# Cross-attention softmax on VectorE straight from PSUM: maximum and subtract without ScalarE's copy, and an earlier division

## The chip, the cores and the metric

The kernel runs on one core of a Trainium2 chip. Its time is the device time of one execution in microseconds (us). A core has TensorE (PE, matrix products into PSUM), VectorE (DVE), ScalarE (ACT), GpSimd (POOL, which works on SBUF only in this kernel) and SyncE (SP, which only issues DMAs). Each engine runs its own instructions in the order in which they stand, and engines wait for each other through semaphores.

## The reference

Four cross-attention models run one after the other on x (8 batches x 256 tokens x 128) and a context (8 x 64 x 64). The third, L2, holds most of the work and is where the change lies: six layers, each with a self-attention, a cross-attention and a feed-forward block, all with 16 heads of 64.

```python
def step(t, p):
    skv, sq, sow, sob, ckv, cq, cow, cob, w1, b1, w2, b2, pg, pb = p
    tn = _ln(t, norm_g, norm_b)
    t = _mha(tn, tn, skv, sq, sow, sob, tgt_mask) + t
    tn = _ln(t, norm_g, norm_b)
    t = _mha(src, tn, ckv, cq, cow, cob, src_mask) + t
    tn = _ln(t, pg, pb)
    t = t + (jax.nn.relu(tn @ w1 + b1) @ w2 + b2)
    return (t, None)
```

In the cross-attention each of the 256 queries of a batch looks at 64 keys per head: scores, mask, softmax over the 64 keys, weighted sum of values, output projection. The softmax subtracts each row's maximum, exponentiates, and divides by the row's sum.

## The kernel before

**Order of the work.** Nothing is scheduled by a tool. The kernel collects small functions with `at(tick, phase, fn)`; at the end it runs through the ticks in order, and in each tick by phase (lines 1312 to 1323), and ties every instruction of PE, DVE, ACT and POOL behind the one before it on the same engine. So a phase number fixes where an instruction stands in its engine's queue. DMAs on SP are outside this order.

**Layers.** A layer of L2 takes 48 ticks. The self-attention has 32, four per batch (`plan_sa`, line 891), and the cross-attention 16 from tick T_ca on, two per batch (`plan_ca`, line 1108), that is one tick per tile of 128 queries. The feed-forward block of batch b follows at T_ca + 2b + 7 (products L1161, activation L1166) and + 9 (products L1178, add L1182). The next layer's self-attention starts at T_ca + 16, and its normalisation and projections some ticks before, so the stages overlap.

**A tile of cross-attention** (`plan_weights_64`, lines 329 to 446, called with a mask) goes through these steps, for a tile that starts in tick k:

| step | place (tick, phase) | engine and line |
|---|---|---|
| scores | k, 1 | PE L356, L363 (mask): 128 x 1024 into PSUM (16 heads x 64 keys) |
| lower | k, 2 | ACT copies to SBUF, L372; DVE row maximum, L374; POOL subtracts, L375 |
| exps | k, 8 | ACT exponential in place, L381 |
| divide | k+1, 2.4 | DVE sum L385 and reciprocal L386; POOL multiplies, L387 |
| turn | k+2, 2.5 | DVE two 32 x 32 block transposes, L395 |
| sums | k+3, 3.0 | PE L429; then DVE adds bias and residual into t, L1145 |

The same function without a mask serves L0 (16 tiles), where exps comes at k+1 and there is no divide.

**Other work in these ticks.** `ahead` (line 843) prepares a normalised, transposed input for each block: moments of each row on DVE (L849 to L855), their scales on POOL (L859, L862), the normalised rows xn either on ACT (L868) or on DVE (L873), then the transposes on PE (L882) and their eviction on ACT (L884). Its argument `on_scalar` picks the engine of xn; with ACT two small instructions more are needed, `mneg` (L855, DVE) and `nm` (L862, POOL). Self-attention passes False (line 1029), cross-attention and feed-forward take True. For batch 0 of the next layer's self-attention xn is at T_ca + 11, phase 2.6, and its transposes in the same tick, phase 7.2; for batch 1 both are at T_ca + 15. Values (L318, evicted by ACT L324) come in even ticks at 3.2, keys of two batches (L1120, evicted by ACT L1126) at 3.7 in every fourth. The next layer's projections (L902, L921) start at T_ca + 12. Its first scores are L939 at T_ca + 16, phase 1, and VectorE's mask, add and row minimum of them L953, phase 2; ACT's exponential of them is L958.

**PSUM.** All PE results go into one pool of four buffers of two banks each (`two_banks`, tag `ps`). A result waits until the reader of the tile that held its buffer before is done: L372 frees the scores, L1145 the sums, L884 the transposes, L324 the values, L953 the self-attention's scores.

Of the kernel before, what the change touches and what calls it, by code (L numbers as in the profile page):

```python
# [12 lines left out]
ALU = mybir.AluOpType  # L13
AX = mybir.AxisListType
PSUM = bass.MemoryType.PSUM

P = 128
B, S, D = 8, 256, 128
M, DM = 64, 64
# [8 lines left out]
def tile_xattn_stack(ctx: ExitStack, tc: tile.TileContext, io, out: bass.AP):  # L28
    nc = tc.nc
# [21 lines left out]
    def tp_tile():  # L51
        return one_bank("tp")
# [4 lines left out]
    def big(tag, bufs=4, shape=(P, 1024), dtype=F32):  # L57

        return heap.tile(list(shape), dtype, tag=tag, name=uniq(tag), bufs=bufs)

    def sb(shape, tag, bufs=2, pool=None):
        return (pool or act).tile(shape, F32, tag=tag, name=uniq(tag), bufs=bufs)

    def sm(shape, tag):
        return small.tile(shape, F32, tag=tag, name=uniq(tag))
# [12 lines left out]
    def column(name):  # L78
        v = io[name]
        t_ = const.tile([v.shape[0], 1], F32, tag=name, name=name)  # L80
        nc.sync.dma_start(out=t_, in_=v.unsqueeze(1))
        return t_
# [71 lines left out]
    norm_g = column("L2_norm_g")  # L154
    norm_b = column("L2_norm_b")
# [129 lines left out]
    def tt(b):  # L285
        return t[:, QT * b : QT * (b + 1), :]
# [7 lines left out]
    def at(tick, phase, fn):  # L294
        plan.setdefault(tick, []).append((phase, fn))
# [33 lines left out]
    def plan_weights_64(tick, qt, qT, keys, values, mask, take):  # L329
# [39 lines left out]
        def lower():  # L369
            sc = tl.pop("sc")  # L370
            e = big("e", shape=(P, 16, M))
            nc.scalar.copy(e.rearrange("p h k -> p (h k)"), sc)  # L372
            m = sm([P, 16], "m16")
            nc.vector.tensor_reduce(m, e, AX.X, ALU.max)  # L374
            nc.gpsimd.tensor_tensor(  # L375
                e, e, m.unsqueeze(2).to_broadcast([P, 16, M]), ALU.subtract
            )
            tl["e"] = e

        def exps():  # L380
# [53 lines left out]

        at(tick, 1, scores)
        at(tick, 2, lower)
        if mask is None:
            at(tick + 1, 2.05, exps)
            at(tick + 1, 2.5, turn)
            at(tick + 2, 1.9, sums_by_head)  # L440
            at(tick + 2, 4.6, outputs)
        else:
            at(tick, 8, exps)
            at(tick + 1, 2.4, divide)
            at(tick + 2, 2.5, turn)
            at(tick + 3, 3.0, sums)

# [235 lines left out]
    def plan_l0(b, T):  # L683
# [88 lines left out]
        for qt in range(QT):  # L772
            plan_weights_64(
                T + qt, qt, lambda: st["q"], lambda: st["k"], lambda: st["VW"], None,
                lambda ps, qt=qt: add(qt, ps),
            )
# [66 lines left out]
    def ahead(b, stats_at, normal_at, tT_at, g, bias, st, on_scalar=True):  # L843

        def moments():
            st["mv"] = sm([P, QT, 2], "mv")
            for j in range(QT):
                six = sm([P, 6], "six")
                nc.vector.bn_stats(six, tt(b)[:, j, :])  # L849
                nc.vector.bn_aggr(st["mv"][:, j, :], six)  # L850
            st["ve"] = sm([P, QT], "ve")
            nc.vector.tensor_scalar(st["ve"], st["mv"][:, :, 1], 1e-5, None, ALU.add)
            if on_scalar:
                st["mneg"] = sm([P, QT], "mneg")
                nc.vector.tensor_scalar(st["mneg"], st["mv"][:, :, 0], -1.0, None, ALU.mult)  # L855

        def scales():
            st["rstd"] = sm([P, QT], "rstd")
            nc.gpsimd.tensor_tensor(st["rstd"], st["ve"], mhalf, ALU.pow)  # L859
            if on_scalar:  # L860
                st["nm"] = sm([P, QT], "nm2")
                nc.gpsimd.tensor_tensor(st["nm"], st["mneg"], st["rstd"], ALU.mult)  # L862

        def normal():
            st["xn"] = sb([P, QT, D], "xn", 3)
            for j in range(QT):
                if on_scalar:
                    nc.scalar.activation(  # L868
                        st["xn"][:, j, :], tt(b)[:, j, :], AF.Identity,
                        scale=st["rstd"][:, j : j + 1], bias=st["nm"][:, j : j + 1],  # L870
                    )
                else:
                    nc.vector.tensor_scalar(  # L873
                        st["xn"][:, j, :], tt(b)[:, j, :], st["mv"][:, j, 0:1],
                        st["rstd"][:, j : j + 1], ALU.subtract, ALU.mult,
                    )

        def trans():
            ps = tp_tile()
            xn = st.pop("xn")  # L880
            for j in range(QT):
                nc.tensor.transpose(ps[:, j * P : (j + 1) * P], xn[:, j, :], ident)  # L882
            st["tT"] = sb([D, S], "tT", 5)
            nc.scalar.activation(st["tT"], ps[:, :S], AF.Identity, scale=g, bias=bias)  # L884

        at(*stats_at, moments)
        at(stats_at[0], 8.4, scales)
        at(*normal_at, normal)
        at(*tT_at, trans)

    def plan_sa(l, b, T):


        st = {"q": [], "k": [], "v": [], "oT": [], "eT": []}
# [131 lines left out]
        def mask():  # L1026
            st["nm"] = load_mask(b)

        ahead(b, (T - 6, 8.3), (T - 5, 2.6), (T - 5, 7.2), norm_g, norm_b, st, False)
        at(T - 2, -1, mask)  # L1030
        at(T - 4, 3.6, lambda: project(W["sa", l][2], "q", HD ** -0.5, 0, False))
        at(T - 4, 3.7, lambda: project(W["sa", l][2], "q", HD ** -0.5, 1, False))
# [75 lines left out]
    def plan_ca(l, b, T):  # L1108
# [38 lines left out]
        for qt in range(QT):  # L1147
            plan_weights_64(
                T + qt, qt, lambda: st["tT"], lambda: keys_of[b], lambda: st["VW"],
                nm2[:, b].unsqueeze(1).to_broadcast([P, 4, M]), lambda ps, qt=qt: add(qt, ps),  # L1150
            )
# [119 lines left out]
    for l in range(NL):  # L1271
        T_ca = T0 + 4 * B
        T_next = T_ca + 2 * B
        for b in range(B):
            plan_sa(l, b, T0 + 4 * b)
        plan_ca_weights(l, T_ca - 6)
        for b in range(B):
            plan_ca(l, b, T_ca + 2 * b)
            T_ff = T_ca + 2 * b + 7
            if l + 1 < NL:  # L1280
                plan_ff(l, b, T_ff, T_ff + 2)
            elif b < B - 2:
                plan_ff(l, b, T_ff, T_ff + 1)
            else:

                T_ff -= b - B + 3
                done = T_ca + 2 * b + 4
                plan_ff(
                    l, b, T_ff, T_ff + 1,
                    (4.6, (done, 6), (done, 8.7), (T_ff, 2.9)),  # L1290
                )
            T_end[b] = T_ff + 1
        if l > 0:
            at(T0 + 8, -1, lambda l=l: load_ff(l))
        if l + 1 < NL:
            at(T_ca + 4, -1, lambda l=l: load_sa(l + 1))
            at(T_next + 1, -1, lambda l=l: load_ca(l + 1))
        T0 = T_next
# [82 lines left out]
```

## Time and profile before

| what | value |
|---|---|
| median of three runs | 2408.54 us (2406.35 to 2409.7) |
| profiled execution | 2410.29 us; its span, first to last instruction, 2408.5 us |
| mean granted TensorE clock in it | 0.987 |
| L372, ACT copy of the scores (128 x 1024) | 112 times, mean 1006 ns |
| L374, DVE maximum | 112 times, mean 1217 ns |
| L375, POOL subtract | 112 times, mean 1902 ns |
| L381, ACT exponential | 112 times, mean 1062 ns |
| L385, L386, DVE sum and reciprocal | 96 times each, mean 1208 and 253 ns |
| L387, POOL multiply | 96 times, mean 1902 ns |
| L873, DVE xn (128 x 128) | 96 times, mean 562 ns |
| L868, ACT xn (128 x 128) | 192 times, mean 492 ns |

Of the 112 tiles 96 belong to the masked cross-attention (6 layers x 8 batches x 2). Busy time counts an engine's instructions from start to end; neighbours overlap a little, so a mean can exceed the advance from one start to the next. The chain of waits follows the work that ended last backwards, at each step to what released it. The timeline lists instructions by start time, runs of equal ones merged, with the idle time before them and its releaser in brackets.

### The profile page before, as it was taken

The numbers are of one execution on the slowest core, as the hardware profiler recorded it, in microseconds if no ns is written. First come the engines' busy times: TensorE is split into PE (matmuls) and PEld (weight loads), VectorE is DVE, ScalarE is ACT, GpSimd is POOL, SyncE is SP. The second block draws the span as 40 slices with busy tenths as digits, with TensorE's granted clock in tenths as the row PEclk, the third lists the DMA queues.
The fourth block names the chain that finished last, engine by engine and source line by source line (L and its number), as shares of the span: only waits on it lengthen the run. The fifth ranks groups of instructions, "written<-read, shape, count | busy, mean of one in ns | idle before, by whom it ended". The sixth has DMA issues, their size and how long they took to land.

```text
span 2408.5 us, 100346 instructions
## 1 busy us (share of the span) xinstructions
PE 2325.2 (97%) x42564; PEld 1719.9 (71%) x42564; DVE 1872.3 (78%) x6237; ACT 1707.7 (71%) x4514; POOL 1359.1 (56%) x2231
## 2 busy tenths in 40 slices
PE   7889999999999999999999999999999999999997
PEld 4557777777777777777777777777777777777775
DVE  5677887777888767888767888767888767888775
ACT  4567777667777667778667778667778667777663
POOL 2444556754556754555764555755555765455665
PEclk9989999999999999999999999999999999999998
DMA  6000022001022001012000012000013000001000
GB/s 180 2 2 20 21 73 65 2 3 30 21 64 66 11 3 30 21 56 73 12 2 26 21 45 87 12 2 18 25 40 89 21 2 18 25 26 42 2 4 16
DMA packets 102834, 76.90 MB, mean 32 GB/s; under 512 B 8113, under 2 KB 96881, under 8 KB 102386
## 3 DMA queue, kind: packets, MB, share of 16 engines
q1 hardware_dynamic: 101794, 70.16, 10.1%
q8 instruction: 335, 5.49, 0.9%
q14 instruction: 113, 0.93, 0.1%
q10 hardware_dynamic: 592, 0.33, 0.1%
HBM read 62.07 MB, written 8.39 MB: 29 GB/s over the span
## 4 chain that ended last, share of the span: by engine, by line
PE 75%; DVE 13%; ACT 5%; POOL 4%; issue 2%; DMA 0%; SPq 0%; POOLq 0%; ACTq 0%; DVEq 0%
PE sc L939 12%; PE mm L902 12%; PE mm L994 12%; PE mm L1012 6%; PE mm L921 6%; PE mm L429 6%; PE sc L356 5%; DVE e L953 3%; PE mm L1178 3%; PE mm L1161 3%; DVE eTc L978 2%; DVE m L374 2%; POOL e L968 2%; PE mm L1120 2%; PE mm L318 2%
## 5 line engine op out<-in xcount | busy, mean ns | idle before, releaser
L968 POOL TENSOR_SCALAR e<-e,rs 128x256 f32<-128x256 f32 x1536 | 702.8, 478 | 706.3 <-DVE rs L966 696.5
L958 ACT ACTIVATE e<-e,mn 128x256 f32<-128x256 f32 x1536 | 758.6, 495 | 151.3 <-DVE mn L953 146.5
L953 DVE CUSTOM_DVE_ANT_0 e<-sc,nm 128x256 f32<-128x256 f32 x1536 | 543.1, 419 | 93.4 <-PE sc L939 92.3
L978 DVE STREAM_TRANSPOSE eTc<-e 128x512 f32<-128x512 f32 x768 | 516.2, 694 | 59.4 <-POOL e L968 58.2
L939 PE MATMUL sc<-k,q 64*32 64x256 f32 x12288 | 380.8, 383 | 2.3 <-DVE o L299 1.3
L994 PE MATMUL mm<-eTc,v 32*64 32x256 f32 x12288 | 363.4, 378 | 5.7 <-ACT AT L1095 3.3
L375 POOL TENSOR_TENSOR e<-e,m 128x1024 f32<-128x1024 f32 x112 | 213.0, 1902 | 262.1 <-DVE m L374 262.1
L994 PEld LDWEIGHTS mm<-eTc,v 32*64 32x64 f32 x12288 | 277.1, 131 | 88.5 <-issue 22.2
L939 PEld LDWEIGHTS sc<-k,q 64*32 64x32 f32 x12288 | 221.8, 107 | 125.3 <-issue 51.4
L374 DVE TENSOR_REDUCE m<-e 128x16 f32<-128x1024 f32 x112 | 136.3, 1217 | 197.0 <-ACT e L372 197.0
L958 ACT ACTIVATION_READ_ACCUMULATOR e<-e,mn 128x1 f32 x1536 | 287.9, 187 | 0.0
L356 PE MATMUL sc<-q,tT 128*32 128x256 f32 x3072 | 217.0, 382 | 3.8 <-DVE t L1019 3.2
L429 PE MATMUL mm<-v,o 128*128 128x128 f32 x1536 | 197.5, 283 | 1.9 <-DVE t L1145 1.7
L429 PEld LDWEIGHTS mm<-v,o 128*128 128x128 f32 x1536 | 183.1, 195 | 19.0 <-issue 9.1
L902 PE MATMUL mm<-tT,w_sk 128*128 128x256 f32 x768 | 189.2, 389 | 0.2 <-PE mm L994 0.2
L1012 PEld LDWEIGHTS mm<-w_sow,o 128*128 128x128 f32 x1536 | 175.1, 192 | 17.6 <-issue 12.3
L921 PE MATMUL mm<-w_sv,tT 128*32 128x256 f32 x3072 | 185.6, 382 | 0.0
L1012 PE MATMUL mm<-w_sow,o 128*128 128x128 f32 x1536 | 183.6, 278 | 1.3 <-ACT WVO L1093 1.3
L387 POOL TENSOR_TENSOR e<-e,r 128x1024 f32<-128x1024 f32 x96 | 182.6, 1902 | 0.5 <-DVE r L386 0.5
L301 ACT COPY v<-mm 128x1024 f32<-128x1024 f32 x96 | 97.1, 1012 | 115.4 <-PE mm L921 115.4
L902 PE MATMUL mm<-tT,w_sq 128*128 128x256 f32 x768 | 173.6, 379 | 0.0
L902 PEld LDWEIGHTS mm<-tT,w_sk 128*128 128x128 f32 x768 | 138.3, 190 | 44.2 <-issue 29.2
(222 smaller groups left out, 3489.4 us busy)
## 6 DMA issues: line engine op xcount, KB each, us to landing
nm<-mask_d SPq DMA_DIRECT2D x192, 128.0 KB
wd<-o SPq DMA_DIRECT2D x48, 128.0 KB
w_sk<-in_L_sa_kv_dram SPq DMA_DIRECT2D x6, 512.0 KB
w_sv<-in_L_sa_kv_dram SPq DMA_DIRECT2D x24, 128.0 KB
w_sq<-in_L_sa_q_dram SPq DMA_DIRECT2D x6, 512.0 KB
w_sow<-in_L_sa_ow_dram SPq DMA_DIRECT2D x6, 512.0 KB
w_ckv<-in_L_ca_kv_dram SPq DMA_DIRECT2D x12, 256.0 KB
w_cq<-in_L_ca_q_dram SPq DMA_DIRECT2D x6, 512.0 KB
```

Source lines behind the costliest of these rows:

```text
L356: nc.tensor.matmul(sc[32 * a : 32 * a + 32, q, :], lhsT=qT()[:, qb * 32 : (qb + 1) * 32], rhs=keys()[:, a].rearrange("p h k -> p (h k)"), ...
L375: nc.gpsimd.tensor_tensor(e, e, m.unsqueeze(2).to_broadcast([P, 16, M]), ALU.subtract)
L429: nc.tensor.matmul(ps[:, :D], lhsT=eT[:, s].rearrange("p q x -> p (q x)"), rhs=vw[:, r, k, g, :], start=(s == 0), stop=(s == 7),)
L902: nc.tensor.matmul(ps[:, i * S : (i + 1) * S], lhsT=w[:, c * P : (c + 1) * P], rhs=st["tT"], start=True, stop=True,)
L921: nc.tensor.matmul(ps[32 * a : 32 * a + 32, i, :], lhsT=st["tT"][:, kb * 32 : (kb + 1) * 32], rhs=sv[:, a].rearrange("p g x -> p (g x)"), ...
L939: nc.tensor.matmul(sc[32 * a : 32 * a + 32, r, j, :], lhsT=st["q"][g][rows, a, qb * 32 : (qb + 1) * 32], rhs=st["k"][g][rows, a, :], start ...
L953: nc.vector.tensor_tensor_reduce(e[:, i, :], sc4[:, i, :], st["nm"][:, 2 * jj + i % 2, :], -1.0, 3.0 * BIG, ALU.add, ALU.min, mn[:, i : i ...
L958: nc.scalar.activation(e[:, i, :], e[:, i, :], AF.Exp, scale=-1.0, bias=mn[:, i : i + 1], accum_out=rs[:, i : i + 1],)
L968: nc.gpsimd.tensor_scalar(e[:, i, :], e[:, i, :], rs[:, i : i + 1], 1.0, ALU.mult, ALU.mult)
L978: nc.vector.transpose(eT[:, r, :, 2 * jj : 2 * jj + 2, :], e[:, 2 * r : 2 * r + 2, :].rearrange("p j (k x) -> p k j x", x=32),)
L994: nc.tensor.matmul(ops[a // 2][r * HD : (r + 1) * HD, a % 2, :S], lhsT=st["v"][kb // 4][rows, kb % 4, (2 * g + r) * HD : (2 * g + r + 1) * ...
L1012: nc.tensor.matmul(st["ps"][:, j * D : (j + 1) * D], lhsT=st["oT"][c // 4][:, c % 4, j * P : (j + 1) * P], rhs=sow[:, c, :], start=(c == 0 ...
```

## The change

For masked tiles `lower` no longer copies the scores to SBUF: VectorE takes the maximum from PSUM and subtracts it from PSUM, writing the difference to SBUF. ScalarE's copy and GpSimd's subtract go. L0's tiles keep the old way. `divide` moves from phase 2.4 of tick k+1 to phase 0.9, ahead of that tick's scores and lower. Batches 0 and 1 of each self-attention get their xn from ScalarE (`b < 2` as `on_scalar`). In the changed program the maximum is L381, the subtract L382, and the lines behind them are 7 higher.

```diff
         def lower():
             sc = tl.pop("sc")
             e = big("e", shape=(P, 16, M))
-            nc.scalar.copy(e.rearrange("p h k -> p (h k)"), sc)
             m = sm([P, 16], "m16")
-            nc.vector.tensor_reduce(m, e, AX.X, ALU.max)
-            nc.gpsimd.tensor_tensor(
-                e, e, m.unsqueeze(2).to_broadcast([P, 16, M]), ALU.subtract
-            )
+            if mask is None:
+                nc.scalar.copy(e.rearrange("p h k -> p (h k)"), sc)
+                nc.vector.tensor_reduce(m, e, AX.X, ALU.max)
+                nc.gpsimd.tensor_tensor(
+                    e, e, m.unsqueeze(2).to_broadcast([P, 16, M]), ALU.subtract
+                )
+            else:
+                sc = sc.rearrange("p (h k) -> p h k", k=M)
+                nc.vector.tensor_reduce(m, sc, AX.X, ALU.max)
+                nc.vector.tensor_tensor(
+                    e, sc, m.unsqueeze(2).to_broadcast([P, 16, M]), ALU.subtract
+                )
             tl["e"] = e
...
         else:
             at(tick, 8, exps)
-            at(tick + 1, 2.4, divide)
+            at(tick + 1, 0.9, divide)
             at(tick + 2, 2.5, turn)
             at(tick + 3, 3.0, sums)
...
-        ahead(b, (T - 6, 8.3), (T - 5, 2.6), (T - 5, 7.2), norm_g, norm_b, st, False)
+        ahead(b, (T - 6, 8.3), (T - 5, 2.6), (T - 5, 7.2), norm_g, norm_b, st, b < 2)
```

## The prediction

> **What bounds the kernel now.** I read the page first, then groups by line, then the timeline of one layer's cross-attention. A tile is 128 queries of one batch; I write tile k and tick k for the k-th of a layer's cross-attention (tick T_ca + k, 16 tiles), and give the times of layer 0, whose tick 0 starts at 396.7 us.
>
> The page's busy shares and its chain that ended last:
>
> ```profile
> PE 2325.2 (97%) x42564; PEld 1719.9 (71%) x42564; DVE 1872.3 (78%) x6237; ACT 1707.7 (71%) x4514; POOL 1359.1 (56%) x2231
> ...
> PE 75%; DVE 13%; ACT 5%; POOL 4%; issue 2%; DMA 0%; SPq 0%; POOLq 0%; ACTq 0%; DVEq 0%
> ```
>
> TensorE carries the chain. Time taken off another engine is worth only the PE idle that goes with it; time put on VectorE costs where PE waits for it. The three groups that the change touches (last columns: busy us, mean ns, idle before and what ended it):
>
> ```profile
> L375 POOL TENSOR_TENSOR e<-e,m 128x1024 f32<-128x1024 f32 x112 | 213.0, 1902 | 262.1 <-DVE m L374 262.1
> ...
> L374 DVE TENSOR_REDUCE m<-e 128x16 f32<-128x1024 f32 x112 | 136.3, 1217 | 197.0 <-ACT e L372 197.0
> ...
> L372 ACT COPY e<-sc 128x1024 f32<-128x1024 f32 x112 | 112.7, 1006 | 50.2 <-PE sc L363 25.4 <-PE sc L343 24.8
> ```
>
> The idle of 262 and 197 us is off the path: the waits view names hardly any PE wait on these lines. PE idles in the cross-attention at two places per layer, shown by the timeline (start, duration, engine, line, idle before). The first is tick 6:
>
> ```profile
> 430.94 1.21 DVE L374 TENSOR_REDUCE m<-e 128x16 f32<-128x1024 f32 x1
> ...
> 433.74 0.93 PE L882 MATMUL tp<-ident,xn 128*128 128x128 f32 x4 [1.19 <-ACT xn L868]
> ...
> 434.64 0.25 DVE L1145 TENSOR_TENSOR t<-mm,tb 128x128 f32<-128x128 f32 x1
> ...
> 434.95 2.95 PE L429 MATMUL mm<-v,o 128*128 128x128 f32 x16 [0.28 <-DVE t L1145]
> ```
>
> VectorE is here some 4 us behind PE: the add L1145 of tile 2 frees the PSUM buffer that tile 3's sums need. The sums then take 2.95 us where others take 2.05, because the windows view has the granted clock (next to last but two) at 0.59 after this idle:
>
> ```profile
> 436.00:440.00 4.00, 4.00 (x49) 2.73 (x50) 3.70 (x6) 1.41 (x4) 2.54 (x3) 0.59 0.00 0
> ```
>
> The second is tick 11, where PE waits for the next layer's first normalisation on VectorE:
>
> ```profile
> 475.97 2.11 DVE L873 TENSOR_SCALAR xn<-t,mv,rstd 128x128 f32<-128x128 f32 x2
> ...
> 477.54 0.30 PE L882 MATMUL tp<-ident,xn 128*128 128x128 f32 x1 [0.88 <-DVE xn L873]
> 478.00 0.28 DVE L1145 TENSOR_TENSOR t<-mm,tb 128x128 f32<-128x128 f32 x1
> 478.13 0.33 PE L882 MATMUL tp<-ident,xn 128*128 128x128 f32 x1 [0.29 <-DVE xn L873]
> ```
>
> **Price of the new operations.** The subtract from PSUM with a broadcast has a near row: L631, 128x1024 from PSUM plus a broadcast, 1.207 us. The maximum from PSUM: L1221 reduces 256 elements from PSUM in 0.41 us, as L502 does from SBUF (0.41), so I take L374's 1.22. Back to back an instruction advances VectorE by 1.14 (424.79 to 425.93), and 1.24 if the next needs its result (425.93 to 427.17). So lower costs VectorE 1.24 + 1.14 = 2.38 us a tile, 1.24 more than before; over 96 tiles +119 us (78% to 83% of the span). ScalarE loses 96 x 1.006 = 97 us, GpSimd 96 x 1.902 = 183 us. Alone this is nothing: 33.9 us of VectorE idle per layer (before L374) could hold the 16 x 1.24 = 19.8 us, if it lay at the right ticks.
>
> The rows L631 and L374 show no surcharge for reading PSUM. [...]
>
> **The walk.** Order on VectorE in tick k becomes: divide(k-1) 1.41, max and subtract(k) 2.38, turn(k-2) 1.17, add(k-3) 0.20, and in even ticks from 4 two sets of moments, 2.26. A pair of ticks costs 12.6 us (before: 10.1). PE needs 9.8 for ticks 4 and 5 (420.38 to 430.17), but about 15.5 once the feed-forward joins (453.3 to 468.8). So VectorE is the slower up to about tick 8 and PE after it. Against that, the loop copy-max-subtract-exp-copy over three engines (1.0 + 1.2 + 1.9 + 1.0) disappears, and subtract ends earlier after the scores.
>
> Ticks 0 to 4: nearly equal. VectorE uses its waits for L372 (0.98, 1.74 and 2.04 us in ticks 0 to 2); add_out L1019, for which the scores of tick 3 wait, stays within 0.4 us.
>
> Tick 4 to 6: divide(3) 423.05 to 424.45, lower(4) to 426.8, turn and add to 428.2, moments to 430.6, divide(4) to 432.05, lower(5) to 434.4, turn(3) to 435.6, add(2) to 435.8. Before, that add ended at 434.89. The sums of tile 3 start **0.9 us later**.
>
> Ticks 7 to 10: divide now stands ahead of lower and waits for exp, which ScalarE runs last in its tick. exp(7) comes behind the feed-forward's four L1166 and an xn (449.98 before, plus 0.9) and ends at 451.8; VectorE, done with tick 7 at 449.85, idles 2 us. Then divide(7) to 453.25, lower(8) to 455.6, turn and add to 457.0, moments to 459.25, divide(8) to 460.65, lower(9) to 463.0. In the changed program's buffer assignment the scores of tick 10 take the buffer of tile 9's scores, and PE is there at 461.1 + 0.9 = 462.0: **1.0 us more**.
>
> Tick 11: the two L873 leave VectorE. ScalarE has xn by about 475.5 (moments to 473.4, scales 0.9, xn 0.9) and the transposes follow at once: from PE's starts (474.71 + 1.78, then 0.37 for two transposes, against 478.39) **1.5 us back**. Batch 1's pair (513.37) stopped no one.
>
> The price of b < 2 besides: mneg 0.16 and nm 0.2 us twice per layer, in the moments above; ScalarE's 0.9 us pairs delay exp(11) by 0.5, under the projections that fill PE in tick 12.
>
> Tick 16, where the next layer's self-attention begins:
>
> ```profile
> 517.37 1.05 ACT L381 ACTIVATE e<-e 128x1024 f32<-128x1024 f32 x1
> 517.43 0.42 DVE L953 CUSTOM_DVE_ANT_0 e<-sc,nm 128x256 f32<-128x256 f32 x1 [1.41 <-PE sc L939]
> ...
> 520.27 1.09 PE L318 MATMUL mm<-WVO,ctx 64*32 64x256 f32 x32
> ```
>
> divide(15) moves ahead of the eight L953 and waits for exp(15), until 517.37 + 1.05 = 518.4; L953 starts 2.4 us later (518.4 + 1.41). The values L318 take the buffer that the first four L953 free, at 521.2 instead of 518.8: about 1.05 us of wait, and 0.35 for the projection behind them: **1.4 us more**. ScalarE's eight L958 and its copies queue behind, but the buffers that they free are wanted later.
>
> Nothing is put on the SP queue; GpSimd's multiply moves forward with divide and passes only residual and scale work.
>
> **Sum.** (0.9 + 1.0) x 6 layers = +11.4; -1.5 x 5 (the last layer has no successor) = -7.5; +1.4 x 5 = +7. The last layer also carries the final stage's VectorE work, 13.3 of 16.1 us busy (2321.65 to 2337.76); with 2.5 more it is nearly full: 0 to +5, I take +1. The granted clock drops in tick 6 of layers 0, 1, 3 and 5 (windows at 436, 804, 1540 and 2278), not of 2 and 4; from tick 6 to tick 7 layer 0 takes 1.25 us longer than layer 2. The longer idle in tick 6 could bring the drop to the two layers without one: +2.5, bounds 0 and +15 (two more drops in each layer). Total +14.4 us.
>
> [...]
>
> The profiled execution took 2410.3 us (span 2408.5); the median of the runs shown is 2408.5. From the median: **2423 us**.
>
> **Rivals.** (A) *Faster.* If the three-engine loop was what held VectorE back, and max plus subtract come out 0.3 us a tile cheaper than 2.38 (three tiles then make up the 0.9 us), VectorE is no longer late in tick 6. The idle there (1.5) and its clock drop (1.25 in four layers) go, tick 10 costs nothing: -9 - 5 - 7.5 + 7 = -14.5, 2394 us. For it: VectorE's 33.9 us of idle per layer. Against it: no gap from 424.79 to 434.89. (B) *Same.* PE's slack hides early delays and tick 16 is caught up in self-attention: about 2408 us, bounds 2404 and 2413. Against: PE is full from 480 to 550. (C) *Slower by the clock.* Each new wait brings a drop: 14.4 + 12 = +26, 2435 us. (D) The copy isn't gone: excluded, the program lists 96 fewer copies.
>
> **Numbers.** Forecast 0.45, A 0.22, B 0.18, C 0.15. A measurement of this kernel can tell about 0.2% (4.8 us) from no change: A is faster, B the same, the rest slower. The range reaches from near A's time to just past C's: 2397 to 2438. The likeliest one's own: 2414 to 2431.
>
> **What would show it.** Right: VectorE waits for exp before divide's sum in ticks 8 and 16; PE waits for the subtract at the scores of tick 10 and for L953's at the values of tick 16, about 1 us each; no PE wait for xn in tick 11; max and subtract 1.2 us each. Wrong: sums of tile 3 that start before 434.95, or a tick 16 without PE idle.

## The result, and the profile after

The changed kernel takes **2418.66 us** (median of six, 2416.57 to 2422.91), the kernel before 2407.77 beside it: a ratio of 1.0046, 95% interval 1.0033 to 1.0059. The forecast was 2423 us, from 2408.5. The profiled execution took 2420.12 us with a span of 2418.1, 9.8 us more than the one of before.

The page of the changed kernel, busy shares and the chain that ended last:

```profile
PE 2327.7 (96%) x42564; PEld 1722.5 (71%) x42564; DVE 1958.0 (81%) x6321; ACT 1629.2 (67%) x4442; POOL 1190.1 (49%) x2147
...
PE 70%; DVE 18%; ACT 5%; POOL 3%; issue 3%; DMA 1%; SPq 1%; ACTq 0%; DVEq 0%; POOLq 0%
```

ScalarE and GpSimd were relieved by 79 and 169 us, and VectorE took 86 more. The chain shows what that is worth: five points of it went from PE to VectorE. The groups by line (busy us, mean ns, idle before and what ended it):

```profile
L382 DVE TENSOR_TENSOR e<-sc,m 128x1024 f32<-128x1024 f32 x96 | 117.5, 1224 | 3.3
L381 DVE TENSOR_REDUCE m<-sc 128x16 f32<-128x1024 f32 x96 | 111.8, 1165 | 0.0
...
L392 DVE TENSOR_REDUCE r<-e 128x16 f32<-128x1024 f32 x96 | 116.5, 1213 | 109.1 <-ACT e L388 109.1
```

The two PSUM operations have the price that was forecast, 1.17 and 1.22 us. VectorE's idle time didn't vanish: it used to stand ahead of the maximum (197 us, for the copy) and now 109 us of it stand ahead of the division's sum, for exp. PE pays in four places, which the waits view names (total us, times, longest); three are new, and the sums L436 waited 1.7 us in all before:

```profile
PE mm L318 <- DVE mn L960: 6.1, 5, 1.2
PE mm L436 <- DVE t L1152: 5.3, 6, 0.9
PE sc L356 <- DVE e L382: 5.3, 5, 1.1
PE tp L889 <- DVE e L382: 5.1, 6, 0.9
```

The first is tick 16, the third tick 10, the other two are tick 6. The timeline of tick 6 in layer 0 (start, duration, engine, line, idle before):

```profile
428.83 0.71 PE L889 MATMUL tp<-ident,xn 128*128 128x128 f32 x2 [0.61 <-ACT xn L875]
...
430.39 0.41 PE L889 MATMUL tp<-ident,xn 128*128 128x128 f32 x2 [0.85 <-DVE e L382]
...
431.69 3.64 PE L436 MATMUL mm<-v,o 128*128 128x128 f32 x16 [0.89 <-DVE t L1152]
```

Three waits, 2.35 us together, where before had 1.47 (1.19 + 0.28): 0.88 more. Behind them the sums run at a lowered clock, as before; the windows view has it at 0.58 (next to last but two):

```profile
431.00:435.00 4.00, 3.31 (x15) 3.31 (x16) 3.93 (x6) 1.25 (x3) 1.81 (x1) 0.58 0.02 4
```

Tick 8 and tick 10:

```profile
447.69 1.22 DVE L392 TENSOR_REDUCE r<-e 128x16 f32<-128x1024 f32 x1 [1.94 <-ACT e L388]
...
457.60 1.22 DVE L382 TENSOR_TENSOR e<-sc,m 128x1024 f32<-128x1024 f32 x1
...
458.97 0.64 PE L356 MATMUL sc<-q,tT 128*32 128x256 f32 x8 [1.05 <-DVE e L382]
```

VectorE stands 1.94 us in tick 8 for exp(7); two ticks later PE waits 1.05 us until the subtract has freed the buffer. Tick 16:

```profile
514.73 1.22 DVE L392 TENSOR_REDUCE r<-e 128x16 f32<-128x1024 f32 x1 [3.92 <-ACT e L388]
...
516.23 0.42 DVE L960 CUSTOM_DVE_ANT_0 e<-sc,nm 128x256 f32<-128x256 f32 x1
...
517.84 1.10 PE L318 MATMUL mm<-WVO,ctx 64*32 64x256 f32 x32 [1.23 <-DVE mn L960]
...
519.22 1.97 PE L909 MATMUL mm<-tT,w_sk 128*128 128x256 f32 x8 [0.28 <-DVE rs L973]
```

The division waits 3.92 us for exp(15), the self-attention's first L960 stand behind it, and PE waits for the buffer that they free. In tick 11 the wait is gone; the transposes L889 follow L1185 at once:

```profile
472.57 1.95 PE L1185 MATMUL mm<-w_f,o 128*128 128x128 f32 x16
...
474.36 0.38 PE L889 MATMUL tp<-ident,xn 128*128 128x128 f32 x2
```

To add it up I matched PE's instructions one by one in the two traces (their order is the same) and took the start of each tick's first L356. How much longer the changed kernel takes from one tick to the next, layers 0 to 5:

| stretch | forecast | measured, us | sum |
|---|---|---|---|
| up to layer 0's cross-attention | 0 | -3.98 | -4.0 |
| ticks 0 to 6 | 0 | -0.33 in each layer | -2.0 |
| tick 6 to 7 | +0.9 x 6, +2.5 for the clock | 1.06, 1.07, 0.71, 1.07, 2.31, -0.51 | +5.7 |
| tick 9 to 10 | +1.0 x 6 | 1.12 x 5, last layer nothing | +5.6 |
| tick 11 to 12 | -1.5 x 5 | -1.58 x 5 | -7.9 |
| tick 15 to the next layer's tick 0 (tick 16 lies in it) | +1.4 x 5 | 1.80, 1.65, 1.65, 2.32, 1.69 | +9.1 |
| the rest of the last layer | +1 | 0.31 + 0.10 + 2.64 | +3.1 |
| all | +14.4 | | +9.6 |

### The profile page after: what moved, and what is told of

Same layout as the page of the kernel before. It is cut to its first block, busy times and chain, and to the rows that moved or that the text cites. A ratio compares the mean times of both kernels' runs of the same rounds, so it can differ in the third digit from the quotient of the medians.

```text
span 2418.1 us, 100403 instructions
## 1 busy us (share of the span) xinstructions
PE 2327.7 (96%) x42564; PEld 1722.5 (71%) x42564; DVE 1958.0 (81%) x6321; ACT 1629.2 (67%) x4442; POOL 1190.1 (49%) x2147
## 4 chain that ended last, share of the span: by engine, by line
PE 70%; DVE 18%; ACT 5%; POOL 3%; issue 3%; DMA 1%; SPq 1%; ACTq 0%; DVEq 0%; POOLq 0%
PE mm L909 12%; PE sc L946 12%; PE mm L1001 11%; PE mm L1019 7%; PE mm L928 6%; PE mm L436 5%; DVE e L960 5%; PE sc L356 4%; PE mm L1185 3%; PE mm L1168 3%; DVE eTc L985 3%; POOL e L975 2%; DVE r L392 2%; DVE m L381 2%; PE mm L1127 1%
## 5 line engine op out<-in xcount | busy, mean ns | idle before, releaser
L960 DVE CUSTOM_DVE_ANT_0 e<-sc,nm 128x256 f32<-128x256 f32 x1536 | 543.3, 419 | 91.6 <-PE sc L946 90.2
L356 PE MATMUL sc<-q,tT 128*32 128x256 f32 x3072 | 217.0, 382 | 5.3 <-DVE e L382 5.3
L392 DVE TENSOR_REDUCE r<-e 128x16 f32<-128x1024 f32 x96 | 116.5, 1213 | 109.1 <-ACT e L388 109.1
L436 PE MATMUL mm<-v,o 128*128 128x128 f32 x1536 | 197.7, 283 | 5.5 <-DVE t L1152 5.3
L436 PEld LDWEIGHTS mm<-v,o 128*128 128x128 f32 x1536 | 183.1, 195 | 23.0 <-issue 7.5
L1019 PEld LDWEIGHTS mm<-w_sow,o 128*128 128x128 f32 x1536 | 175.1, 192 | 17.2 <-issue 12.3
L1019 PE MATMUL mm<-w_sow,o 128*128 128x128 f32 x1536 | 183.6, 278 | 1.2 <-ACT WVO L1100 1.2
L866 POOL TENSOR_TENSOR rstd<-ve,mhalf 128x2 f32<-128x2 f32 x144 | 100.8, 700 | 121.9 <-DVE mneg L862 108.2
```

The source lines that it names most:

```text
L356: nc.tensor.matmul(sc[32 * a : 32 * a + 32, q, :], lhsT=qT()[:, qb * 32 : (qb + 1) * 32], rhs=keys()[:, a].rearrange("p h k -> p (h k)"), ...
L436: nc.tensor.matmul(ps[:, :D], lhsT=eT[:, s].rearrange("p q x -> p (q x)"), rhs=vw[:, r, k, g, :], start=(s == 0), stop=(s == 7),)
L960: nc.vector.tensor_tensor_reduce(e[:, i, :], sc4[:, i, :], st["nm"][:, 2 * jj + i % 2, :], -1.0, 3.0 * BIG, ALU.add, ALU.min, mn[:, i : i ...
L1019: nc.tensor.matmul(st["ps"][:, j * D : (j + 1) * D], lhsT=st["oT"][c // 4][:, c % 4, j * P : (j + 1) * P], rhs=sow[:, c, :], start=(c == 0 ...
```

## The experiments

My theory after the result: the early division makes ticks 10 and 16 late, VectorE's load tick 6, and the third edit (xn of two batches on ScalarE) gives tick 11 back. The rivals were that load makes tick 10 late, and that tick 11's gain comes from somewhere else. Times are medians; the kernel before beside them took 2409.9, 2409.5 and 2409.7 us in the three groups of runs. Per-tick numbers are from matched traces as above.

**e1_late_divide**: the changed kernel, with

```diff
-            at(tick + 1, 0.9, divide)
+            at(tick + 1, 2.4, divide)
```

> The changed kernel with the division back at its old place (phase 2.4, behind lower). Theory: the waits at the scores of tick 10 (1.12 us in five layers) and in tick 16 (about 1.65 us in five layers) come from the early division alone, which waits for exp in front of the subtract and of the self-attention's first scores. Both go: -5.6 - 8.3, from 2418.7 to about 2405 us; tick 6 keeps its later start (+1.1 us per layer), since VectorE's load is the same. Rival (load): the 1.24 us that lower adds per tile make tick 10 late; then that wait stays and only tick 16 goes, about 2410 us. Rival (neither): with the division later, turn and sums are late and it stays at 2418.

2404.21 us, ratio to before 0.9974 (0.9963 to 0.9985). Against the changed kernel, tick 10 loses 1.12 us in each of five layers, and the stretch into the next layer 1.61 to 1.92; tick 6 keeps +0.75 to 0.78 over before (where the clock did not differ). So neither wait arises without the early division, and load alone doesn't make tick 10 late. The two edits without the early division are faster than the kernel before.

**e5_late_last**: the changed kernel, only tile 15's division late.

```diff
-            at(tick + 1, 0.9, divide)
+            at(tick + 1, 2.4 if n == 15 else 0.9, divide)
```

> The changed kernel with only the division of a layer's last tile (tile 15, which falls into tick 16) back at phase 2.4; the other fifteen stay early. Theory: tick 16's cost belongs to that one division, which stands ahead of the self-attention's first VectorE work: tick 16 loses about 1.65 us in five layers (-8.3), tick 10 keeps its 1.12 us: 2418.7 to about 2410.4 us. Rival: tick 16 is late because the whole train of early divisions leaves VectorE and ScalarE behind by then; then tick 16 keeps half of it or more, 2414 us or more.

2411.49 us. The stretch into the next layer loses 1.61 to 1.94 us, as much as with all divisions late, and tick 10 stays to 0.00. Tick 16 is the doing of one instruction at the seam of two layers.

**e2_no_xn**: the changed kernel, with

```diff
-norm_g, norm_b, st, b < 2)
+norm_g, norm_b, st, False)
```

> The changed kernel with the self-attention's normalised rows of all batches on VectorE again (False in place of b < 2). Theory: the 1.58 us that tick 11 gained in five layers, and two waits of 1.1 us less ahead of the first layer, are due to this edit alone: +7.9 + 2.2, about 2428.8 us. Rival: part of the gain comes from GpSimd being idler (the rows on VectorE are quick once GpSimd's subtract is gone: 0.5 instead of 1.05 us each); then the time is 2420 to 2424 us.

2419.57 us, 1.0041 of the kernel before beside it, where the changed kernel has 1.0046: beside the other two edits the third is worth nothing that stands out from the noise. My theory falls: tick 11 takes 0.10 us longer, not 1.58. Yet the same edit alone on the kernel before is worth its full price:

**e3_xn_only**: the kernel before with `False` replaced by `b < 2`.

> The kernel before with only the third edit (ScalarE makes the normalised rows of batches 0 and 1). Theory: the gain stands by itself, -7.9 - 2.2: 2407.8 to about 2397.7 us. Rival: ScalarE still has its copies here, 1.0 us per tile, so the rows come later on it and less than half is left: 2403 us or more.

2400.32 us, ratio 0.9960 (0.9945 to 0.9975); tick 11 gains 1.58 us in five layers. So tick 11's wait has two remedies, each sufficient, and the changed kernel has both. The second shows in the rows themselves. In the kernel before GpSimd's multiply starts 0.56 us ahead of them (the prediction shows their line, 475.97):

```profile
475.41 1.90 POOL L387 TENSOR_TENSOR e<-e,r 128x1024 f32<-128x1024 f32 x1
```

The timeline of the kernel without the third edit (e2_no_xn), tick 11, then of the kernel with only the first edit (e7_lower_only, below):

```profile
472.10 1.90 POOL L394 TENSOR_TENSOR e<-e,r 128x1024 f32<-128x1024 f32 x1 [0.95 <-DVE r L393]
...
473.96 0.73 POOL L305 TENSOR_TENSOR tb<-t,w_fb 128x256 f32<-128x256 f32 x1
...
475.43 0.56 DVE L880 TENSOR_SCALAR xn<-t,mv,rstd 128x128 f32<-128x128 f32 x2
```

```profile
480.69 1.24 DVE L402 STREAM_TRANSPOSE o<-e 128x512 f32<-128x512 f32 x2
480.92 1.90 POOL L394 TENSOR_TENSOR e<-e,r 128x1024 f32<-128x1024 f32 x1 [3.17 <-DVE r L393]
...
481.85 1.73 DVE L880 TENSOR_SCALAR xn<-t,mv,rstd 128x128 f32<-128x128 f32 x2
482.77 0.72 POOL L305 TENSOR_TENSOR tb<-t,w_fb 128x256 f32<-128x256 f32 x1
483.04 0.30 PE L889 MATMUL tp<-ident,xn 128*128 128x128 f32 x1 [1.76 <-DVE xn L880]
```

The two rows take 0.56 us where GpSimd is idle and 1.73 beside its multiply; by the single records the first ends at 482.90, just behind the multiply (482.82), the second at 483.58, just behind the residual add L305 (483.50). In the kernel before they took 2.11 us. With the division early and no subtract on GpSimd, its multiply is over before the rows begin.

**e7_lower_only**: the kernel before with only the new `lower`.

> The kernel before with only the first edit (maximum and subtract from PSUM); the division late, no third edit. The kernel without the third edit kept tick 11's gain of 1.58 us, so that wait has two remedies: VectorE's rows leave VectorE, or GpSimd doesn't run a long instruction beside them (the pair of rows took 2.11 us beside GpSimd's multiply in the kernel before, 0.56 us with GpSimd idle there). Theory: with the division late, GpSimd's multiply overlaps the rows again, but its subtract is gone: tick 11 gains only 0.5 to 1.3 us, tick 6 costs 0.77 us, the head is as before: about 2410 us. Rival (early division is all): tick 11 is as in the kernel before, about 2414 us. Rival (the subtract is all): tick 11 gains its full 1.58 us, about 2406 us.

2426.96 us, ratio 1.0070 (1.0055 to 1.0085), slower than all three guesses. The late division's multiply covers the rows again, and they start later, behind VectorE's subtract: PE waits 1.76 us and tick 11 costs 0.88 us more than before. In four layers a drop of the clock follows this wait as well, 1.5 to 1.7 us in tick 12. I had not thought of that.

**e4_divide_only**: the kernel before with `at(tick + 1, 0.9, divide)`.

> The kernel before with only the division moved to the front of the next tick. Theory: tick 16 costs the same 1.65 us in five layers as in the changed kernel (+8.3), tick 10 nothing, since there ScalarE's copy and not VectorE frees the scores; GpSimd's multiply now stands ahead of its subtract, and the loop copy, maximum, subtract, exp grows by the division, which makes tick 6 about 1.5 us later in six layers (+9): 2425 us, between 2416 (tick 16 alone) and 2432. Rival: the early division does no harm without the subtract on VectorE, 2408 us.

2419.04 us, ratio 1.0039 (1.0025 to 1.0054). The stretch into the next layer costs 1.52 to 1.65 us, as forecast, tick 10 nothing, also as forecast. Tick 6 is 0.72 us later in the two layers in which neither kernel has a drop of the clock, half of what I expected, and 0.5 us earlier in three where this kernel is rid of the drop; 0.77 us appear in tick 2, which I had not expected: the scores of tick 3 wait for the add L1019, behind the early division on VectorE, 7.9 us in the six layers instead of 3.2. The rows of tick 11 take 2.47 us here, beside the subtract, which now comes after the multiply:

```profile
474.44 1.90 POOL L375 TENSOR_TENSOR e<-e,m 128x1024 f32<-128x1024 f32 x1
474.64 2.47 DVE L873 TENSOR_SCALAR xn<-t,mv,rstd 128x128 f32<-128x128 f32 x2
```

They start earlier than before, so tick 11 gains 0.36 us in five layers, but the early division alone doesn't free them. Seven of the eight combinations of the edits (the early division with xn was not run):

| lower | early division | xn | us |
|---|---|---|---|
| | | | 2409.9 |
| x | | | 2427.0 |
| | x | | 2419.0 |
| | | x | 2400.3 |
| x | x | | 2419.6 |
| x | | x | 2404.2 |
| x | x | x | 2418.7 (before beside it: 2407.8) |

The kernel before took 2409.5 to 2409.9 us beside all of these but the last. The xn edit is worth 9.6 us alone, 22.8 beside the new `lower`, and nothing that can be told beside both others. The new `lower`, the main part of the change, gains in no pair of rows: it costs 17.1 us alone, 3.9 beside xn and 0.6, within the noise, beside the early division.

**e8_pool_busy**: e2_no_xn, and in five layers

```diff
+        def more():
+            for _ in range(4):
+                nc.gpsimd.tensor_tensor(idle, idle, idle, ALU.mult)
+
+        if l and b == 0:
+            at(T - 5, 2.55, more)
```

> The changed kernel without the third edit, and with four extra GpSimd multiplies (128 x 256 on a scratch tile, about 1.9 us together) right before batch 0's normalised rows on VectorE in tick 11 of five layers. Theory: VectorE's pair of rows stretches again from 0.56 to about 1.5 to 2.1 us while GpSimd runs, PE waits for it in tick 11 again, by 1.0 to 1.6 us in five layers: 2419.6 to about 2426 us. Rival: GpSimd's work does not touch VectorE, and tick 11 stays as it is, 2419.6 us.

2429.51 us. Timeline of tick 11:

```profile
474.43 2.69 POOL L1041 TENSOR_TENSOR idle<-idle 128x256 f32<-128x256 f32 x4
...
475.90 1.30 DVE L882 TENSOR_SCALAR xn<-t,mv,rstd 128x128 f32<-128x128 f32 x2
```

The rows stretch from 0.56 to 1.30 us and tick 11 takes 0.74 us longer in five layers. GpSimd does hold VectorE's rows up, by less than I guessed: the multiplies begin 1.47 us ahead of the rows, and the rows end at 476.51 and 477.20, just behind the third and fourth of them (476.43 and 477.12). That accounts for 3.7 of the 9.9 us. In the profiles most of the rest is the clock's, in tick 6 (three drops of 6.8 us in layers 0, 2 and 4 here, three of 3.4 us in 1, 3 and 5 of e2_no_xn) and at the end; whether the extra work moved the drops or chance did stays open.

**Tick 6.** If VectorE's load were all, the new path in the first three tiles alone, where VectorE only waits, should help. **e6_first_three**: e1_late_divide with

```diff
-            if mask is None:
+            if mask is None or n > 2:
                 nc.scalar.copy(e.rearrange("p h k -> p (h k)"), sc)
```

> Maximum and subtract from PSUM on VectorE for the first three tiles of each layer's cross-attention alone, the old copy on ScalarE and subtract on GpSimd from the fourth on; the division late as before; the third edit kept. Theory (load): VectorE is late in tick 6 by its work of ticks 3 to 5, 1.24 us more per tile on the new path, while in ticks 0 to 2 it only waits for the copies (0.98, 1.74 and 2.04 us). So tick 6 loses the 0.77 us that the new path costs there, and some 1 us of the idle of before; with the clock drop gone in some layers 2388 to 2394 us, against 2400.3 with the third edit alone and 2404.2 with the new path for all tiles. Rival: what VectorE saves in the first ticks comes back as a wait for the copy of the fourth tile: tick 6 as before, 2400 us.

2397.92 us. The rival is right: tick 6 is as in the kernel before (to 0.01 us in five layers). Against e1_late_divide it does lose the 0.77 us that the new path cost, so these belong to the tiles from the fourth on. What VectorE saves before them counts for nothing, because it stands still at the fourth tile's maximum, in this kernel as in e3_xn_only (line L374 there, also 3.51 us). The timeline of e6_first_three:

```profile
416.49 1.22 DVE L375 TENSOR_REDUCE m<-e 128x16 f32<-128x1024 f32 x1 [3.51 <-ACT e L374]
```

So VectorE's lateness in tick 6 arises behind this wait, and there two sets of moments fall into tick 4 back to back. One of them can be had earlier. **e9_xn_stats** is e3_xn_only with the moments of the cross-attention's normalisation in tick T - 5; **e10_late_stats** is e1_late_divide with the same, **e11_three_stats** e6_first_three with the same:

```diff
-        ahead(b, (T - 4, 6), (T - 3, 2.95), (T - 2, 2.9), norm_g, norm_b, st)
+        ahead(b, (T - 5, 6), (T - 3, 2.95), (T - 2, 2.9), norm_g, norm_b, st)
```

> The kernel before with the third edit, and the moments for the cross-attention's normalisation one tick earlier (T - 5 in place of T - 4, so that the two sets no longer fall into the same even tick). Theory: in tick 6 PE waits because VectorE is late after two sets of moments in tick 4; in tick 3 it waits 1.3 to 3.5 us for copies anyway. Taking one set (1.2 us) out of tick 4 starts tick 6's sums up to 1.2 us earlier in six layers (-7), and spares the clock drop in those layers that have one (-1.2 each): from 2400.3 to 2388 to 2394 us. Rival: the set only moves the wait, since the loop copy, maximum, subtract, exp is as long as before: 2400 us.

> The changed kernel with the division late, and the moments one tick earlier as in the run beside it. Theory (load): with maximum and subtract on VectorE that engine has no idle time in ticks 3 to 6, so the set of moments moved to tick 3 delays the add of tick 5 by just as much as in tick 4, unless tick 2's idle (2.5 us before the maximum of tick 3) takes it in: there it does, so tick 6 gains 1.2 us in six layers here too: from 2404.2 to about 2397 us, 2392 with the clock drops gone. Rival: no gain where VectorE is full, 2404 us.

> First three tiles of each layer on the new path, the others on the old, the division late, the third edit, and the moments one tick earlier. Theory: it adds the 1.2 us of tick 6 in six layers to 2397.9: 2386 to 2392 us, the best of all. Rival: as for the first of these runs, 2398 us.

| kernel | us | ratio to before |
|---|---|---|
| e9_xn_stats | 2384.15 | 0.9898 (0.9882 to 0.9915) |
| e11_three_stats | 2391.46 | 0.9924 (0.9909 to 0.9939) |
| e10_late_stats | 2401.99 | 0.9971 (0.9961 to 0.9980) |

The fastest does without the new path: old `lower`, old division, xn on ScalarE for two batches, moments a tick earlier. Its timeline in tick 6, then the windows view (length; PE, PEld, DVE, ACT, POOL busy; granted clock, DMA share, GB/s):

```profile
428.67 0.66 PE L882 MATMUL tp<-ident,xn 128*128 128x128 f32 x4
...
430.23 2.05 PE L429 MATMUL mm<-v,o 128*128 128x128 f32 x16 [0.90 <-DVE t L1145]
```

```profile
430.00:434.00 4.00, 3.77 (x60) 3.12 (x62) 3.79 (x10) 3.02 (x5) 3.42 (x4) 1.00 0.00 0
```

PE waits 0.90 us instead of 1.47 there, and the clock stays at 1.00. Against the kernel before, tick 6 gains 1.26 us in the two layers that had no drop and 2.50 in the four that had one, another 0.56 in ticks 1 and 2. Of the 1.26, 0.57 are these waits, 0.29 a wait at the scores of tick 7 that is gone, and most of the rest are transposes that run back to back. The forecast had no term for ticks 1 and 2, and the time lies 3.9 us below its range. On the new path the same shift is worth 2.2 us in all: VectorE is full there, and of the 2.2 us that tick 6 gains per layer 0.9 come back in tick 5 and 0.4 in ticks 1 and 2. I had expected nearly as much there as on the old path; the rival, no gain where VectorE is full, is nearer. e11_three_stats lies in its range, but isn't the best of all: the shift gives it the same 1.26 us in tick 6 and takes 0.43 us per layer in ticks 1 and 2.

## Why the prediction was right, and where it was not

- **Price of the operations**: right. 1.17 and 1.22 us from PSUM, where the maximum took 1.22 from SBUF.
- **Tick 6, +0.9**: right in size, 0.88 us of wait, and in part in mechanism. The sums of tile 3 do wait for the add, 0.89 us instead of 0.28. But the transposes ahead of them wait 0.85 us for a PSUM buffer that the subtract L382 frees, which the prediction didn't have, and their wait for xn fell from 1.19 to 0.61. **The clock, +2.5**: wrong. Four layers have a drop, as before; layer 4 gained one (2.31), layer 5 lost one (-0.51).
- **Tick 10, +1.0**: right, by the chain described (exp(7), division, subtract(9), buffer): 1.12 us. It occurs in five layers and not in six: in the last, tick 8 lasts 9.4 us instead of 5.8, with work of the final stage in it, and PE finds the buffer free at tick 10.
- **Tick 11, -1.5**: the size was right, 1.58, the cause incomplete. "The two L873 leave VectorE" is one remedy; the other, which I didn't see, is that the early multiply and the missing subtract leave GpSimd idle beside them. That tick 11 takes only 0.10 us longer in e2_no_xn shows it. I read the 2.11 us of that pair in the profile and took it as given, though the mean of the same line was 562 ns an instruction.
- **Tick 16, +1.4**: right in mechanism, 1.23 us for the buffer and 0.28 for the projection; the whole stretch costs 1.65 in most layers, and the rest of it isn't resolved; no drop of the clock lies in these stretches.
- **What had no term**: the third edit works also ahead of layer 0, where xn stands before the L713 of the earlier models: two waits of PE there fell from 3.2 to 2.1 and from 1.6 to 0.5 us (-2.2), in each profile with the edit that I compared (e1, e3, e6, e9) and in neither e2 nor e4. The rest of the -3.98 I can't assign to an edit; the same stretch varies from +2.6 us (e7) to -3.0 (e8) in profiles without the edit. Ticks 0 to 6 gained 0.33 us per layer, which I had called nearly equal.
- **The last layer, +1**: 3.1 measured, and not by VectorE's load. 2.64 of it lie behind tick 15, where the clock is lowered for 16.8 us in the kernel before and for 20.4 in the changed one (by the traces' clock records). e2_no_xn, with no less work on VectorE, has 13.2 us of lowered clock there and takes 0.85 us less than before.
- **Rival A** (the loop over three engines holds VectorE back): wrong for tick 6. Without the loop in the first three tiles nothing changes there, and on the old path, loop and all, a shifted set of moments takes 1.26 us and the clock's drop out of it.
- **Rival C** (each new wait brings a drop): wrong here. In the changed kernel's cross-attention all drops lie in tick 6; none follows the waits of ticks 10 and 16 (1.05 and 1.23 us in layer 0). In e7_lower_only one follows the longer wait of tick 11 (1.76 us) in four layers.

So 2423 came out 4.3 us high, and it is that near in part by luck: in the profiles the time up to layer 0 (-4.0), tick 6 with its clock (-2.2) and ticks 0 to 6 (-2.0) came out below the forecast, the seams and the last layer (+2.1 each) above it. The sign was no luck: it rests on the two ticks that the early division delays, and both were forecast by their mechanism.

## What to carry to other kernels

An operation that is moved forward in an in-order queue brings its wait along: what stood behind it waits too, and here that was a buffer release two ticks later (1.05 us of PE's time) and the first work of the next stage (1.23 us). Edits that remove the same wait don't add up: run each alone and in pairs before any of them is given the credit. And where one instruction takes four times its usual time (here 1.43 us for 0.31), ask what ran beside it before moving it.

## What the runs showed of the hardware

**Some of VectorE's instructions ended with GpSimd's, others kept their times.** In the profile before, 38 of the 96 rows of L873 (128x128 TENSOR_SCALAR) begin while GpSimd runs nothing and take 0.31 us each. The other 58 begin while a GpSimd instruction runs, take 0.50 to 1.43 us, and each ends 0.08 to 0.09 us behind it (477.39 after 477.31, 478.08 after 478.00). In e4_divide_only the first of tick 11 took 1.78 us beside a subtract, and ended at 476.42 after 476.34. The division's sum L385 lies in 90 of its 96 cases for over half of its time beside a subtract or multiply on GpSimd, and took 1.21 us there, 1.19 in the other six. A block transpose of L395 took 0.66 us beside them and 0.67 without.

**Where the clock was lowered.** Between 200 and 2300 us the profiles of before and after each show four stretches at half the clock, one in tick 6 of four layers, each 3.413 us long. By the traces' clock records their starts (before: 435.90, 804.54, 1541.82 and 2279.10; after: 431.63, 803.68, 1544.38 and 1916.43) lie whole multiples of 3.413 us apart. Cut into pieces of this length from these starts, the two profiles have PE busy for a share of 0.55 (before) and 0.31 to 0.49 (after) in the piece just ahead of a lowered stretch, and for 0.57 or more in every piece that none follows. The waits in tick 6 of the changed kernel's layer 0 (2.35 us) lie, but for 0.06 us, in a piece with 0.31 (a drop followed); in tick 6 of layer 2 no piece is below 0.62 (none followed). In the kernel before the two layers without a drop had 0.57 and 0.58. From tick 6 to tick 7 the layers 0, 1 and 3, with a drop, took 1.22 to 1.25 us longer than layer 2 in the kernel before, and 1.58 to 1.59 in the changed one. Layers 2 and 4 of e8_pool_busy, with drops of 6.8 us, took 2.8 us longer than those of e2_no_xn, which have none.

**The maximum took about as long from PSUM as from SBUF.** For 128x1024 it took 1.165 us from PSUM in the changed kernel and 1.219 in e1_late_divide, and from SBUF 1.217 in the kernel before and 1.179 in e4_divide_only.
